# Four of nine taps of three depthwise 3x3 convolutions move from TensorE to VectorE in the overlapped stages

## Chip, cores and metric

The kernel runs on one core of a Trainium2 chip. The metric is the device time of one launch in microseconds (us); for the kernel before, the median of 3 runs is 12007.12 us (11998.74 to 12011.87).

## What is computed

The input is x, eight images of 64 channels and 64 x 64 pixels in float32. Four blocks follow one another. Each of the last two has parts that don't matter here; what matters are three depthwise 3x3 convolutions (one 3x3 filter for each channel):

```python
# block 0: attention over all 4096 pixels, then
out = conv3x3_depthwise(out, w2); out = relu(bn2(out)); out = bn3(conv1x1(out, w3)) + x
# block 1: two layers of attention in 8x8 windows, each with an MLP
# block 2: nine spatially weighted taps, a 1x9 convolution, a residual
# block 3: a selective scan (state space model) over four directions
xc = silu(conv3x3_depthwise(xi, conv_w) + conv_b)      # 128 channels
h = h * exp(dt * A) + dt * B * xc; y = sum(h * C)      # along 4096 pixels, 16 states, 4 directions
# block 3, last part: the channels in four groups i, each max-pooled by 2**i,
# each with a 3x3 depthwise convolution (mfr_w, mfr_b), upsampled, joined, then
out = gelu(conv1x1(joined, aggr_w) + aggr_b) * x
```

## The kernel before

Two images are handled together as a pair, on 128 partitions (2 images x 64 channels); a tile of one pair is 128 x 4096 and is worked on in eight chunks of 512 columns (8 rows of 64 pixels). There are four pairs. For each, the *front* (L1282) computes blocks 0 to 2 and, in `scan_sources` (L1645), the inputs of the scan; the *scan* (L1713) follows; the *back* (L1882) makes the output from the scan's result, the pyramid of pooled convolutions being its second half.

The stages overlap. The front of pair 0 runs by itself (about 0 to 1530 us). Then, beside the scan of pair p, run the back of pair p-1 and the front of pair p+1. The scan of pair 3 has the back of pair 2 beside it, and the back of pair 3 partly beside it and partly behind it. The front and back are Python generators that yield a cost; `scans` records scan steps and takes from the generators in proportion. The program's order sets only the priorities: a scheduler puts the instructions on each engine's queue, each engine then works its queue in order.

A scan has 512 steps, each with two of the sixteen states of 512 columns. A step is: two row broadcasts by DMA (B and C, L1801); on POOL (GpSimd) a product of 128 x 1024 (`vd<-B,du`, L1809); on ScalarE (ACT) two exponentials (`dad`, L1831) and copies of the carried ends (L1842); on VectorE (DVE) two scans (`hd` or `dad`, L1834); the product with C, on POOL or DVE (L1845, L1848); and on TensorE (PE) two sums (`yd<-vd`, L1860), each over half of PE's columns. Eight steps share two products of input rows (`pdd`, `pbc`, L1771 and L1779).

A depthwise tap on PE is a product with a diagonal 128 x 128 matrix made by `spread_taps` (L1249). `taps_sum` (L1269) makes a chunk: taps 0 to n-1 on PE into one PSUM bank, the others as multiply-adds on DVE into the same bank:

```python
            if t < n:
                nc.tensor.matmul(dst, lhsT=diag[:, t], rhs=src, start=(t == 0), stop=stop and t == n - 1)
            else:
                nc.vector.scalar_tensor_tensor(dst, src, wt[:, t : t + 1], dst, ALU.mult, ALU.add)
```

It is used at three places. In `layer0` (L1364) the bank `cacc` is read by ACT (L1366), goes through a 1x1 product on PE (`pw`, L1368), ACT again, and is added to X on DVE (L1371). In `scan_sources` (L1672), for each of the two images of a pair, the bank `xacc` is read by ACT with Silu (L1674), copied to XT (L1675), and stored by DMA (L1676). At both, n is 5 while a front is alone (pair 0) and 9 in the three others. In the back (L1975), the first level of the pyramid of pairs 0 to 2 has all nine taps on PE, with the 1x1 weights `agT` folded into the diagonal matrices, so that the bank `pa` holds that level's part of the joined sum directly; three products with the upsampled other levels follow (L1979), then Gelu on ACT (L1986), two DVE instructions (L1987, L1988), and the store. For the last pair (`alone` in `back`) all nine taps are on DVE. PSUM banks come from rings of three: `f` for the front and back, `da` for the scan; in the last scan the back alternates between the two.

Of the kernel before, what the change touches and what calls it, by code (L numbers as in the profile page):

```python
# [9 lines left out]
F32 = mybir.dt.float32  # L10
AF = mybir.ActivationFunctionType
ALU = mybir.AluOpType
# [5 lines left out]
P = 128  # L18
# [4 lines left out]
TAPS = 9  # L23
# [1136 lines left out]
class _Direct:  # L1160
# [127 lines left out]
    def layer0(self, p):  # L1288


        nc, tc, w, net, half = self.nc, self.tc, self.w, self.net, self.HALF
        X = self.flat("X")
        nc.sync.dma_start(X, self.net.x[2 * p : 2 * p + 2].rearrange("b c h w -> (b c) (h w)"))
        att = self.padded("att")
        VT = self.flat("VT").rearrange("p (t c) -> p t c", c=P)

        def at(rows, t):
            return X[rows, t * P : (t + 1) * P]

        with self.work("w0") as wk:  # L1300
            for g in range(8):
                pv = self.bank("pval", (P, 4, P))
                nc.tensor.matmul(pv, lhsT=net.ones[0:1, :], rhs=net.b1row.rearrange("o a c -> o (a c)").unsqueeze(1).to_broadcast([1, 4, P]), start=True, stop=False)
                for j in range(4):
                    nc.tensor.matmul(pv[:, j, :], lhsT=at(slice(0, P), 4 * g + j), rhs=net.w1bd, start=False, stop=(j == 3))
                nc.scalar.activation(VT[:, 4 * g : 4 * g + 4, :], pv, AF.Relu)
                yield 3

            parts = wk.tile([P, 2, 32, NCH], F32, name="parts", tag="parts", bufs=1)
            self.dense = 1  # L1310
            for jc in range(NCH):
                po = self.total("po")

                def weigh(t, es):
                    for im in range(2):
                        nc.tensor.matmul(  # L1316
                            po[half[im]], lhsT=VT[:, t, half[im]], rhs=es[im], start=(t == 0), stop=(t == 31)
                        )

                last = None  # L1320
                for t in range(32):
                    ss = [self.bank(f"s{im}") for im in range(2)]
                    for im in range(2):
                        nc.tensor.matmul(  # L1324
                            ss[im], lhsT=at(half[im], t), rhs=X[half[im], jc * CH : (jc + 1) * CH], start=True, stop=True
                        )
                    es = []
                    for im in range(2):
                        e = wk.tile([P, CH], F32, name="e", tag="e", bufs=5)
                        nc.scalar.activation(  # L1330
                            e, ss[im], AF.Exp, scale=C**-0.5, accum_out=parts[:, im, t, jc : jc + 1]
                        )
                        es.append(e)
                    if last is not None:
                        weigh(*last)
                    last = (t, es)
                    yield 3.6
                weigh(*last)
                nc.vector.tensor_copy(self.rows(att, jc), self.img(po))  # L1339

            self.dense = 0
            sums = net.sums[:, p]
            nc.vector.tensor_reduce(sums, parts, AX.X, ALU.add)
            rec = wk.tile([P, 2, 32], F32, name="rec", tag="rec", bufs=1)
            nc.vector.reciprocal(rec, sums)
            for g in range(8):
                pr = self.bank("prec")
                for j in range(4):
                    for im in range(2):
                        nc.tensor.matmul(  # L1350
                            pr[half[im], j * P : (j + 1) * P],
                            lhsT=rec[:, im, 4 * g + j : 4 * g + j + 1].to_broadcast([P, 64]),
                            rhs=w["ident"],
                            start=True,
                            stop=True,
                        )
                d = self.rows(att, g)
                nc.vector.tensor_tensor(d, d, self.img(pr), ALU.mult)
                yield 3
        with self.work("w0b") as wk:  # L1360
            diag = self.spread_taps(wk, w["dw2"])
            for c in range(NCH):
                acc = self.bank("cacc", (P, 8, 64))
                yield from self.taps_sum(acc, diag, att, 8 * c, 1.56, wt=w["dw2"], n=5 if self.alone else TAPS)  # L1364
                cv = wk.tile([P, 8, 64], F32, name="cv", tag="cv")
                nc.scalar.activation(cv, acc, AF.Relu, scale=net.bn23[:, 0:1], bias=net.bn23[:, 1:2])  # L1366
                pw = self.bank("pw")
                nc.tensor.matmul(pw, lhsT=w["w3bd"], rhs=cv, start=True, stop=True)  # L1368
                nc.scalar.activation(pw, pw, AF.Identity, scale=net.bn23[:, 2:3], bias=net.bn23[:, 3:4])
                x = X[:, c * CH : (c + 1) * CH]  # L1370
                nc.vector.tensor_tensor(x, x, pw, ALU.add)  # L1371
                yield 2.25
        return X
# [271 lines left out]
    def scan_sources(self, p, X2):  # L1645

        nc, tc, w, net, half = self.nc, self.tc, self.w, self.net, self.HALF
        x2 = self.memory("x2")
        with tc.tile_pool(name="w3", bufs=2) as wk:
            H = self.flat("H3")  # L1650
            diag = self.spread_taps(wk, w["cw"])
# [7 lines left out]
            for im in range(2):  # L1659
                xc, xt, zs = self.memory("xc"), self.memory("xt"), self.memory("zs")  # L1660
                pad = self.padded("XI")
                for c in range(NCH):
                    pi = self.bank("pi")
                    nc.tensor.matmul(
                        pi, lhsT=w["inT"][half[im], 0:P], rhs=H[half[im], c * CH : (c + 1) * CH], start=True, stop=True
# [3 lines left out]
                XT = self.flat("XT").rearrange("p (w h) -> p h w", h=64)  # L1669
                for c in range(NCH):  # L1670
                    acc = self.bank("xacc", (P, 8, 64))
                    yield from self.taps_sum(acc, diag, pad, 8 * c, 1.5, wt=w["cw"], n=5 if self.alone else TAPS)  # L1672
                    cv = wk.tile([P, 8, 64], F32, name="xcv", tag="xz")
                    nc.scalar.activation(cv, acc, AF.Silu, bias=w["cb"])  # L1674
                    last = nc.scalar.activation(XT[:, 8 * c : 8 * c + 8, :], cv, AF.Copy)  # L1675
                    nc.scalar.dma_start(xc[:, c * CH : (c + 1) * CH], cv.rearrange("p a b -> p (a b)"))  # L1676
                    yield 1.4
# [5 lines left out]
                for c in range(NCH):  # L1683
# [3 lines left out]
                        lhsT=w["inT"][half[im], P : 2 * P],  # L1687
# [194 lines left out]
    def back(self, p):  # L1882
# [3 lines left out]
        F = self.padded("F")  # L1886
# [23 lines left out]
        with tc.tile_pool(name="w5", bufs=1) as wk:  # L1910
            prev, n, ups = F, 64, []
            alone = p == B // 2 - 1
            for i in range(1, 4):
# [40 lines left out]
                ups.append(up)  # L1954
                prev = pool
                yield 7
            ab = w["aggr_b"]
            if not alone:
                near = self.spread_taps(wk, w["mw"][:, 0, :], w["agT"][:, 0, :])
                pm = self.bank("pmb")  # L1960
                nc.tensor.matmul(pm[:, 0:1], lhsT=w["agT"][:, 0, :], rhs=w["mb"][:, 0:1], start=True, stop=True)
                ab = wk.tile([P, 1], F32, name="ab", tag="ab")
                nc.vector.tensor_tensor(ab, pm[:, 0:1], w["aggr_b"], ALU.add)
            for c in range(NCH):
                cols = slice(c * CH, (c + 1) * CH)
                if alone:
                    acc = self.bank("sacc", (P, 8, 64))
                    yield from self.dwconv(acc, F, 8 * c, 8, w["mw"][:, 0, :], w["mb"][:, 0:1])
                    S = wk.tile([P, 8, 64], F32, name="S", tag="S", bufs=2)
                    nc.scalar.activation(S, acc, AF.Copy)  # L1970
                    pa = self.bank("pa", (P, 8, 64))
                    nc.tensor.matmul(pa, lhsT=w["agT"][:, 0, :], rhs=S, start=True, stop=False)  # L1972
                else:
                    pa = self.bank("pa", (P, 8, 64))
                    yield from self.taps_sum(pa, near, F, 8 * c, 1.5, stop=False)  # L1975
                for i in range(1, 4):
                    k = 2**i
                    r = 8 // k
                    nc.tensor.matmul(  # L1979
                        pa,  # L1980
                        lhsT=w["agT"][:, i, :],
                        rhs=ups[i - 1][:, c * r : (c + 1) * r, :].unsqueeze(2).to_broadcast([P, r, k, 64]),
                        start=False,
                        stop=(i == 3),
                    )
                last = nc.scalar.activation(pa, pa, AF.Gelu, bias=ab)  # L1986
                nc.vector.tensor_tensor(pa, pa, self.rows(F, c), ALU.mult)  # L1987
                nc.vector.tensor_tensor(X[:, cols], X[:, cols], pa.rearrange("p a b -> p (a b)"), ALU.add)  # L1988
                nc.sync.dma_start(out[:, cols], X[:, cols])
                yield 3.5  # L1990
# [52 lines left out]
```

## Time and profile before

| | us |
|---|---|
| median of 3 runs | 12007.12 |
| the profiled execution | 12011.7 |
| its span, first to last instruction | 12009.9 |
| front of pair 0 alone | about 0 to 1530 |
| layer-0 convolution, fronts 1, 2, 3 | 2533.6 to 2629.0; 5463.5 to 5563.1; 8346.1 to 8444.6 |
| scan-source convolutions, fronts 1, 2, 3 (two images each) | 3890.5 to 4088.3; 6778.4 to 6970.6; 9660.1 to 9853.8 |
| first pyramid level, backs of pairs 0, 1, 2 | 4462.2 to 4546.3; 7348.9 to 7433.0; 10533.2 to 10688.1 |
| last sum of the scan of pair 3 | 11894 |

Three rows of the page show the course of the span in 40 slices of 300 us, busy tenths for an engine and granted tenths of full clock for PEclk:

```profile
PE   9977999998888779998788978999877986675656
...
DVE  0033367767778474666777555666777748989998
...
PEclk9998989999989889999998989999999987786677
```

A group's line reads: line, engine, operation, written tile <- read tiles, shapes and count | busy us in sum, mean ns of one | idle time of that engine just before, and what ended it. An fp32 product appears as two MATMUL records. Granted clock is the share of TensorE's full clock.

### The profile page before, as it was taken

To read this page: it belongs to the slowest core of one execution; us is meant where nothing else is said; L and a number is where in the kernel's file an instruction comes from. 1 tells how busy PE (TensorE), PEld (TensorE's weight loads), DVE (VectorE), ACT (ScalarE), POOL (GpSimd) and SP (SyncE) were. 2 spreads that over 40 slices of the span, in tenths; PEclk is the share of its full clock that TensorE was granted. 3 is DMA by queue.
4 is the path that set the end of the run, shared out by engine and by line. 5 is a ranking of instruction groups with operands and counts; after the bars stand their busy time and mean duration, and the time that the engine had idled before them with its cause. 6 is when DMAs were issued, how large, how long until landed. Compare 5 with 4: busy or idle time off the path is not lost. (4 is left out here: it accounts for less than half of the span.)

```text
span 12009.9 us, 161406 instructions
## 1 busy us (share of the span) xinstructions
PE 9980.9 (83%) x56180; PEld 3350.9 (28%) x56180; DVE 7806.3 (65%) x8943; ACT 6974.8 (58%) x16029; POOL 7487.9 (62%) x3843
## 2 busy tenths in 40 slices
PE   9977999998888779998788978999877986675656
PEld 2244322233322223223342223222333221121111
DVE  0033367767778474666777555666777748989998
ACT  5555367756665555665665554665666455565554
POOL 0000066668778573666877774566778758888994
PEclk9998989999989889999998989999999987786677
DMA  0000055545445553444444553444444446666663
GB/s 20 1 2 4 33 154 150 148 132 145 134 127 161 157 175 91 136 142 121 147 118 133 150 175 113 127 136 134 135 131 139 128 153 191 185 194 200 206 202 122
DMA packets 779773, 1577.04 MB, mean 131 GB/s; under 512 B 89280, under 2 KB 89408, under 8 KB 778176
## 3 DMA queue, kind: packets, MB, share of 16 engines
q1 hardware_dynamic: 736320, 1443.18, 40.2%
q10 hardware_dynamic: 42624, 123.44, 3.6%
q8 instruction: 444, 7.27, 0.3%
q14 instruction: 385, 3.15, 0.1%
HBM read 1197.16 MB, written 100.66 MB: 108 GB/s over the span
## 5 line engine op out<-in xcount | busy, mean ns | idle before, releaser
L1809 POOL TENSOR_TENSOR vd<-B,du 128x1024 f32<-128x1024 f32 x2048 | 4792.9, 2358 | 2802.6 <-DMA B<-rows 1797.4
L1860 PE MATMUL yd<-vd,pack 128*64 128x512 f32 x8192 | 2705.0, 705 | 668.8 <-POOL vd L1848 466.5
L1831 ACT ACTIVATE dad<-du,As 128x512 f32<-128x512 f32 x4096 | 2721.3, 682 | 697.0 <-DVE hd L1834 331.6
L1834 DVE TENSOR_TENSOR_SCAN hd<-dad,carry,vd 128x512 f32<-128x512 f32 x1989 | 2491.0, 1269 | 529.7 <-ACT dad L1831 471.4
L1848 POOL TENSOR_TENSOR vd<-hd,C 128x512 f32<-128x512 f32 x1293 | 1642.0, 1274 | 818.0 <-DVE hd L1834 816.8
L1834 DVE TENSOR_TENSOR_SCAN dad<-dad,carry,vd 128x512 f32<-128x512 f32 x1595 | 2011.5, 1276 | 184.4 <-ACT dad L1831 181.2
L1845 POOL TENSOR_TENSOR vd<-hd,C 128x1024 f32<-128x1024 f32 x488 | 1149.9, 2356 | 765.9 <-DVE hd L1834 362.7
L1330 ACT ACTIVATE e<-s 128x512 f32<-128x512 f32 x2048 | 1200.1, 591 | 623.4 <-PE s L1324 621.7
L1324 PE MATMUL s<-X 64*128 64x512 f32 x4096 | 1455.6, 647 | 85.5 <-ACT e L1330 66.0
L1848 DVE TENSOR_TENSOR vd<-dad,C 128x512 f32<-128x512 f32 x1827 | 1212.4, 677 | 130.0 <-ACT carry L1842 98.2
L1860 PEld LDWEIGHTS yd<-vd,pack 128*64 128x64 f32 x8192 | 617.5, 154 | 2403.4 <-issue 1152.3
L1316 PE MATMUL po<-e,VT 128*64 128x512 f32 x4096 | 1210.3, 627 | 19.3 <-ACT e L1330 16.2
L1842 ACT ACTIVATE carry<-dad 128x1 f32<-128x1 f32 x1597 | 267.1, 169 | 776.8 <-DVE dad L1834 684.0
L1324 PEld LDWEIGHTS s<-X 64*128 64x128 f32 x4096 | 400.6, 187 | 1129.3 <-issue 840.7
L1842 ACT ACTIVATE carry<-hd 128x1 f32<-128x1 f32 (+1 forms) x1559 | 308.8, 201 | 660.3 <-DVE hd L1834 649.4
L1483 PE MATMUL w_av<-wide,vals 64*32 64x64 f32 x16384 | 494.9, 227 | 116.6 <-DVE w_oc L1512 77.8
L1483 PEld LDWEIGHTS w_av<-wide,vals 64*32 64x32 f32 x16384 | 406.9, 113 | 272.2 <-issue 151.7
L1316 PEld LDWEIGHTS po<-e,VT 128*64 128x64 f32 x4096 | 235.7, 136 | 850.5 <-issue 570.8
L1243 PE MATMUL pv<-n_sq,pack 128*128 128x512 f32 x576 | 347.7, 687 | 148.8 <-ACT n_sq L1241 138.6
L1494 PE MATMUL w_av<-wide,each 64*32 64x128 f32 x8192 | 465.5, 282 | 6.6 <-issue 6.6
L1471 ACT ACTIVATE wide<-wide 128x512 f32<-128x512 f32 x512 | 311.5, 628 | 269.9 <-DVE wide L1470 269.9
L1339 DVE COPY att<-po 128x512 f32<-128x512 f32 x32 | 22.0, 686 | 682.8 <-PE po L1316 682.3
(259 smaller groups left out, 11629.5 us busy)
## 6 DMA issues: line engine op xcount, KB each, us to landing
B<-rows SPq DMA_DIRECT2D x2048, 256.0 KB, 3.6
C<-rows SPq DMA_DIRECT2D x2048, 256.0 KB, 3.6
du<-du SPq DMA_DIRECT2D x384, 512.0 KB, 5.8
du<-du ACTq DMA_DIRECT2D x128, 512.0 KB, 5.1
xs<-xt SPq DMA_DIRECT2D x128, 256.0 KB, 3.9
xs<-xc SPq DMA_DIRECT2D x128, 256.0 KB, 3.7
xc<-xcv ACTq DMA_DIRECT2D x64, 256.0 KB, 2.0
xt<-XT ACTq DMA_DIRECT2D x32, 512.0 KB, 6.1
```

What stands on the lines that cost most here:

```text
L1316: nc.tensor.matmul(po[half[im]], lhsT=VT[:, t, half[im]], rhs=es[im], start=(t == 0), stop=(t == 31))
L1324: nc.tensor.matmul(ss[im], lhsT=at(half[im], t), rhs=X[half[im], jc * CH : (jc + 1) * CH], start=True, stop=True)
L1330: nc.scalar.activation(e, ss[im], AF.Exp, scale=C**-0.5, accum_out=parts[:, im, t, jc : jc + 1])
L1483: nc.tensor.matmul(self.av[rows, 0, x % 4 + j], lhsT=net.vals[half[im], x + j, 4 * g + h], rhs=es[g][half[im], j, h], tile_position=(64 * ...
L1494: nc.tensor.matmul(self.av[rows, 1, x % 4 : x % 4 + 2], lhsT=net.each[half[im], 32 - HD - HD * h : 64 - HD - HD * h], rhs=es[g][half[im], ...
L1809: self.nc.gpsimd.tensor_tensor(v, self.twice(st["B"]), self.units[i // 8]["du"][:, :, 1], ALU.mult)
L1831: nc.scalar.activation(da, u["du"][:, j, 0], AF.Exp, scale=net.As[:, k, n : n + 1])
L1834: nc.vector.tensor_tensor_scan(along(to), along(da), along(v[:, j]), first, ALU.mult, ALU.add)
L1842: nc.scalar.activation(cs, ends, AF.Copy)
L1845: st["w"] = nc.gpsimd.tensor_tensor(v, h, self.twice(CC), ALU.mult)
L1848: m = engine.tensor_tensor(v[:, j], hs[j], CC, ALU.mult)
L1860: m = nc.tensor.matmul(u["y"][self.HALF[j]], lhsT=w["fold"], rhs=st["v"][:, j], start=(i % 8 == 0), stop=(i % 8 == 7))
```

## The change

At the first two places n becomes 5 in all fronts: taps 0 to 4 stay on PE, taps 5 to 8 become multiply-adds on DVE. In the backs of pairs 0 to 2 the first level's taps 0 to 3 are made on DVE in a tile S in SBUF (a share of `big`, one buffer), the bias `mb` going in with the first; taps 4 to 8 stay on PE with the folded matrices; S goes through one product with `agT` into the same bank. The bias of the folded form (one product `pmb` and one small addition) goes. Costs yielded to `scans` stay the same in sum.

```diff
-                yield from self.taps_sum(acc, diag, att, 8 * c, 1.56, wt=w["dw2"], n=5 if self.alone else TAPS)
+                yield from self.taps_sum(acc, diag, att, 8 * c, 1.56, wt=w["dw2"], n=5)
...
-                    yield from self.taps_sum(acc, diag, pad, 8 * c, 1.5, wt=w["cw"], n=5 if self.alone else TAPS)
+                    yield from self.taps_sum(acc, diag, pad, 8 * c, 1.5, wt=w["cw"], n=5)
...
-            ab = w["aggr_b"]
             if not alone:
                 near = self.spread_taps(wk, w["mw"][:, 0, :], w["agT"][:, 0, :])
-                pm = self.bank("pmb")
-                nc.tensor.matmul(pm[:, 0:1], lhsT=w["agT"][:, 0, :], rhs=w["mb"][:, 0:1], start=True, stop=True)
-                ab = wk.tile([P, 1], F32, name="ab", tag="ab")
-                nc.vector.tensor_tensor(ab, pm[:, 0:1], w["aggr_b"], ALU.add)
...
                 else:
+                    S = self.img(self.share(big, 3))
                     pa = self.bank("pa", (P, 8, 64))
-                    yield from self.taps_sum(pa, near, F, 8 * c, 1.5, stop=False)
+                    for t in range(TAPS):
+                        tap = F[:, 8 * c + t // 3 : 8 * c + t // 3 + 8, t % 3 : t % 3 + 64]
+                        wt = w["mw"][:, 0, t : t + 1]
+                        if t == 0:
+                            nc.vector.tensor_scalar(S, tap, wt, w["mb"][:, 0:1], ALU.mult, ALU.add)
+                        elif t < 4:
+                            nc.vector.scalar_tensor_tensor(S, tap, wt, S, ALU.mult, ALU.add)
+                        else:
+                            nc.tensor.matmul(pa, lhsT=near[:, t], rhs=tap, start=(t == 4), stop=False)
+                        if t % 3 == 2:
+                            yield 1.5
+                    nc.tensor.matmul(pa, lhsT=w["agT"][:, 0, :], rhs=S, start=False, stop=False)
...
-                last = nc.scalar.activation(pa, pa, AF.Gelu, bias=ab)
+                last = nc.scalar.activation(pa, pa, AF.Gelu, bias=w["aggr_b"])
```

## The prediction

> **What bounds the kernel now.** I read the page first (busy shares), then the busy time of the stretches in which the edited convolutions run, then the waits in one of them, and then stretches of window attention, which tell what a scan step costs when it must share TensorE.
>
> ```profile
> PE 9980.9 (83%) x56180; PEld 3350.9 (28%) x56180; DVE 7806.3 (65%) x8943; ACT 6974.8 (58%) x16029; POOL 7487.9 (62%) x3843
> ```
>
> TensorE (PE) is the busiest engine, but 83% of a span with several stages does not say where it is the limit. The edited stretches do (columns: start and end, length, then busy us and instructions of each engine, granted clock, DMA share, GB/s). In order: the layer-0 convolution of the second front (2531 to 2630) and the third (5463 to 5564), the two images of a scan-source convolution (6778 on), and the pyramid's first level in the back of pair 1 (7347) and of pair 2 (10530).
>
> ```profile
> core 0: us, PE busy (x) PEld busy (x) DVE busy (x) ACT busy (x) POOL busy (x), PEclk, DMA share, GB/s
> 2531.00:2630.00 99.00, 94.33 (x225) 33.45 (x221) 44.52 (x47) 35.54 (x76) 62.10 (x30) 0.97 0.36 105
> 5463.00:5564.00 101.00, 93.69 (x212) 33.84 (x212) 48.20 (x49) 38.32 (x83) 56.30 (x28) 0.97 0.38 110
> ...
> 6778.00:6858.00 80.00, 80.00 (x202) 29.98 (x200) 36.10 (x35) 46.42 (x75) 45.77 (x23) 1.00 0.45 132
> 6898.00:6971.00 73.00, 73.00 (x183) 28.37 (x181) 21.19 (x22) 33.56 (x52) 32.01 (x16) 1.00 0.27 80
> ...
> 7347.00:7434.00 87.00, 86.63 (x205) 37.64 (x203) 31.07 (x41) 25.71 (x42) 8.66 (x6) 1.00 0.25 75
> 10530.00:10688.00 158.00, 142.33 (x370) 46.29 (x370) 137.34 (x155) 110.48 (x220) 127.41 (x69) 0.98 0.61 187
> ```
>
> In all but the last, PE works 93 to 100% and VectorE (DVE) under half. The last is another regime: DVE 87%, POOL 81%, PE 90%. The waits between 6778 and 6971 say the same; the scan's own sums queue behind taps (engine and line that waited, for whom, us in total, times, longest):
>
> ```profile
> PEld xacc L1275 <- issue: 70.4, 259, 0.8
> DVE xs L1878 <- PE yd L1860: 60.3, 3, 27.9
> ACT xcv L1674 <- PE xacc L1275: 50.7, 8, 7.1
> ```
>
> **Prices.** A full product is two records; in the pyramid 12 products make a chunk, and the gelu product L1987 recurs every 10.30 us there: 0.858 us a product. A scan step's two sums run side by side (yd records start in pairs 0.43 us apart), so a step costs PE 0.86 us, with 1/8 of its two input products 1.07. A step costs DVE about 2.8 us (third front: 48.2 less 4.8 for L1371, over 15.5 steps) and POOL 4.2 (2.36, and 2.36 or 1.27 in turn). Taps on DVE are in the first front's rows: 0.756 each, four in a row 3.13 us (L1277, source in SBUF, accumulator in PSUM).
>
> **Layer-0 convolution (L1364), three fronts.** Removed: 8 chunks x 4 taps x 0.858 = 27.5 us of PE in each; added: 8 x 3.13 = 25 us of DVE. The instruction order of the two builds (counting yd sums between the first and last tap) shows a side effect: the convolution spans 13 scan steps before and 29 after in the second front, 12 and 24 in the other two; by the end of the first attention block both builds stand at the same step. So 16, 12, 12 steps move forward out of the layer norm and first block. In the new stretch PE no longer rules: with 29 steps DVE needs 114 us by its listed order (59 scans at 1.2, 32 taps, the rest at 0.6), POOL 29 x 4.2 = 121; with 24, DVE 107. I take 120, 108 and 108 for 99, 101 and 99: +37 us. What are the moved steps worth where they left? The trace has the experiment: the same block of eight window rows with different numbers of steps (four yd records to a step):
>
> ```profile
> core 0: us, PE busy (x) PEld busy (x) DVE busy (x), PEclk, DMA share, GB/s
> 2725.00:2989.50 264.50, 62.36 (x208) 13.03 (x206) 6.60 (x7) 0.92 0.48 141
> ...
> 5655.50:5905.60 250.10, 59.12 (x194) 12.93 (x194) 6.87 (x7) 0.94 0.47 137
> 6062.60:6299.40 236.80, 52.50 (x162) 11.20 (x162) 7.09 (x6) 0.95 0.42 118
> ```
>
> From 208 to 162 records is 11.5 steps and 27.7 us, 2.4 each; from 194 to 162, 1.7. At 2.0, 40 steps give back 80 us. Net -43. Ends: 1.07 a step (PE's share alone) gives -6; 2.4 gives -59.
>
> **Scan-source convolution (L1672), six images.** Per image PE falls by 27.5 us to 52.5 in the first stretch and 45.5 in the second; DVE rises by 25, to 61 in the first. ACT gets more table loads: the order of the new build alternates Silu and Exp more often, 34 more loads over the six images at 1.28 us (the ACT_TABLE_LOAD rows), 7 an image: 54 and 41 in this front. No engine is full any more. The trace's stretches without a full engine run their largest engine at about 86% (window block at 3149: PE 217.8 of 252.7). So 61 / 0.86 = 71 for 80 us, and in the second image, with DVE, the largest, at 46 to 53 in the three fronts (52 taken), 60 for 73: -9 and -13, three times, -66. Ends: 0, if the chain PE, DVE, ACT is as slow as PE was, and -120, if the largest engine fills.
>
> **Pyramid, first level, backs of pairs 0 and 1 (L1975).** 12 products a chunk become 9: 7.72 for 10.30 us, 8 chunks, -20.6 each. The single S buffer adds a wait: the first tap of the next chunk waits for the product on S, then DVE needs 2.77 us (0.54 for the first, between the rows of L436 at 256 and 1024 elements, 3 x 0.74 from L438), while PE still has three upsampled products and five taps, 6.9 us. That hides it, except in the second and fourth chunk, where up to seven scan instructions are listed between its taps: about 2 us each. -17 each, -34, less 3 for the port below: -31. Ends -40 and -8. The dropped bias product and its 4.0 us wait (L1963) I cost at nothing: PE sets the start of the stretch.
>
> **Back of pair 2, in the last scan.** PE was not the limit, so 24 products less buy nothing; 8 x 2.77 = 22 us of DVE are added where it is 87% busy. And here S matters: three taps in four read F and S, both in SBUF, and the first writes SBUF from SBUF. The row nearest to that is the pooling maximum, both inputs in SBUF:
>
> ```profile
> L1918 DVE TENSOR_TENSOR big<-pool x8: 285/1779/2717, 4426.5 to 11937.7; 128x512 f32<-128x512 f32 x4, 128x128 f32<-128x128 f32 x4
> ```
>
> The 512-element form takes 0.69 us with POOL idle (at 11924) and 2.71 beside three POOL products (at 4426), each of which also grew from 2.36 to 2.5 to 2.8. The Trainium skill (SBUF — State Buffer, "SBUF: two separate sides") has the reason, an exclusive lock on a port pair shared by DVE and POOL, taken by DVE instructions with two SBUF inputs or in a two-port mode; whoever starts first keeps it to the end. By the rule a tap arriving at random waits half a POOL instruction four times in five, 0.8 us: 32 x 0.8 = 26. By the row, 2.0 each: 65. Scans stand between many taps, so I take 1.0: 32. Then (22 + 32) x 0.87 = +48. Ends +15 and +85. The taps into PSUM have one SBUF input and are free of this: L1619, of that kind, stays at 0.75 us beside POOL.
>
> A second rule speaks against the change: TensorE: Matmul & The Clock Gate, "What's actually happening": the clock is full only while PE was recently busy. The row: granted 1.00 in the saturated stretches, 0.92 to 0.95 in the window blocks (85% busy), 0.67 between 10700 and 11500 (58%). With 0.87 the first scan-source stretch needs 52.5 / 0.87 = 60 us of PE, still under 71; by the rule, no idle window, 52.5. Neither changes the sum; up to +20 goes into the range.
>
> **Sum.** -43 - 66 - 31 + 48 = -92. The profiled execution took 12011.7 us (span 12009.9), so 11919.7; the median of the runs shown is 4.6 below that execution: 11915.
>
> **The rivals.** *Given back* (0.12 for within 0.2%, some 24 us, about what a measurement here can tell): moved steps are worth 1.07, the scan-source chain takes its 80 us: -6 + 0 - 31 + 48 = +11, 12018. For it: ACT waits and table loads. Against: DVE and ACT stand under 60% there. *Half* (0.14): cover as computed, but only half of the first two gains, -37, 11970.
>
> *DVE's queue held by TensorE* (0.18, slower): each chunk's first DVE tap waits for its fifth product, and behind it in DVE's queue stand scans, for which POOL and then PE's sums wait. In the first front, with nothing else on PE, DVE waited 1.2 us a chunk (L1277 <- PE xacc). With sums between the products, which wait for POOL up to 6.6 us, I take 2.5: 72 chunks x 2.5 = 180, -92 + 180, about 12100. It decides from 1.3 us a chunk (92 / 72), and is measurable from 1.6. Against it: the scheduler lists scans between taps, and three banks let a chunk's products run ahead.
>
> That the change does nothing is excluded by the order: 4 of 9 tap products are gone from 72 chunks, 3 net in the pyramid. The first front and last back are untouched. *More* (0.06): largest engines fill, 11820.
>
> The likeliest case, 11915, has 0.50, with 11860 to 11965 its own. Faster 0.50 + 0.14 + 0.06 = 0.70, same 0.12, slower 0.18. The range 11830 to 12040 leaves out the slower rival and most of "more".
>
> **What would show it.** Right: the scan-source stretches at 58 to 74 us with PE under 85%; layer-0 stretches longer but the blocks after them 20 to 30 us shorter; the chunk period of the first two pyramids 7.7 us; in the third, S taps of 1.5 us and more. Wrong: DVE idle on PE cacc or PE xacc of over 100 us in sum, or window blocks that don't shrink.

## The result, and the profile after

The changed kernel takes 11917.2 us (median of 4 runs, 11911.3 to 11936.5) against 12004.4 us (4 runs, 11998.7 to 12011.9): ratio 0.9928, 95% interval 0.9916 to 0.9941, some 87 us less. The prediction said 11915. The sum was right to a few us; its terms were not, and the experiments below show which.

First the busy shares of the page of the changed kernel, then the layer-0 convolution of fronts 1 and 2 and the pyramid's first level in the backs of pairs 1 and 2, from the first tap to the last. The columns are those of the same view before.

```profile
span 11913.0 us, 160345 instructions
...
PE 9652.2 (81%) x55454; PEld 3219.2 (27%) x55454; DVE 8095.3 (68%) x9324; ACT 7056.3 (59%) x16085; POOL 7496.5 (63%) x3843
```

```profile
core 0: us, PE busy (x) PEld busy (x) DVE busy (x) ACT busy (x) POOL busy (x), PEclk, DMA share, GB/s
2523.40:2657.50 134.10, 98.21 (x242) 28.80 (x242) 119.25 (x132) 70.84 (x158) 132.19 (x65) 0.86 0.57 174
5405.00:5535.30 130.30, 92.09 (x226) 31.70 (x226) 109.82 (x122) 64.23 (x131) 113.04 (x56) 0.85 0.54 162
...
7257.50:7324.30 66.80, 63.99 (x148) 27.64 (x148) 47.81 (x64) 27.53 (x38) 6.13 (x5) 1.00 0.29 90
10409.70:10587.60 177.90, 131.71 (x314) 41.15 (x312) 165.76 (x173) 103.75 (x200) 126.99 (x66) 0.87 0.52 159
```

Read each against its row before. Layer 0 (first two rows) became longer, 134 and 130 us for 95 and 100, and PE is no longer full: 73% and 71%, at a granted clock of 0.86 and 0.85. The pyramid of pair 1 fell from 84 to 66.8 us with PE still 96% busy. The pyramid of pair 2 grew from 155 to 178, with DVE at 93%.

The scan sources of front 2 are cut at the same three points in both kernels: the first image's convolution, the stretch between the images (the projections `pz` and `pi` and their ScalarE steps), and the second image's convolution. Before, then after:

```profile
core 0: us, PE busy (x) PEld busy (x) DVE busy (x) ACT busy (x) POOL busy (x), PEclk, DMA share, GB/s
6778.40:6855.10 76.70, 76.70 (x194) 29.27 (x193) 33.73 (x32) 43.63 (x72) 42.88 (x21) 1.00 0.45 131
6855.10:6896.00 40.90, 31.84 (x53) 9.96 (x53) 8.87 (x13) 25.50 (x37) 19.17 (x10) 0.65 0.69 217
6896.00:6970.60 74.60, 74.60 (x183) 29.23 (x184) 22.30 (x22) 35.08 (x55) 32.92 (x16) 0.98 0.27 79
```

```profile
6714.10:6766.80 52.70, 50.96 (x133) 17.81 (x132) 47.67 (x56) 39.03 (x60) 35.13 (x18) 1.00 0.59 176
6766.80:6819.50 52.70, 38.02 (x48) 9.63 (x48) 17.10 (x20) 34.98 (x51) 26.93 (x14) 0.52 0.44 147
6819.50:6868.00 48.50, 48.50 (x125) 17.49 (x124) 43.96 (x53) 42.82 (x60) 32.94 (x16) 1.00 0.48 148
```

The convolutions fell by 24 and 26 us, about the 27.5 us of products that left PE. PE is still the full engine in them (97 and 100%), at full clock; DVE now stands at 90 and 91%. The stretch between the images did not shrink: it grew by 12 us, at a lower clock.

The window blocks that stood for the price of a scan step now hold fewer steps (160 and 146 records for 208 and 194) and are shorter, 236 and 221 us for 264 and 250. Then three of the longest waits of the scan sources of front 2 (6682 to 6868). The 60 us of `xs` waiting for PE's sums are down to 2 between first and last tap. The second line is idle time of the weight loads between products; it fell with their number, 133 for 259, and is 0.27 us each as before:

```profile
core 0: us, PE busy (x) PEld busy (x) DVE busy (x), PEclk, DMA share, GB/s
2732.50:2968.70 236.20, 48.96 (x160) 10.40 (x160) 5.23 (x5) 0.93 0.41 122
5622.90:5844.40 221.50, 43.95 (x146) 9.57 (x146) 5.03 (x5) 0.95 0.37 107
```

```profile
POOL vd L1845 <- DVE hd L1834: 45.5, 7, 11.1
PEld xacc L1275 <- issue: 36.0, 133, 0.8
DVE hd L1834 <- ACT dad L1831: 32.8, 17, 9.0
```

The same points of both traces give the course of the gain, each between instructions that both kernels have, before then after:

| | front 1 | front 2 | front 3 | sum of differences |
|---|---|---|---|---|
| layer 0 convolution and first attention block (last attention sum to last projection) | 471.8, 460.3 | 456.0, 453.5 | 448.9, 457.6 | -5.3 |
| scan sources (their diagonals to the back's first norm) | 310.4, 287.3 | 298.0, 268.0 | 299.6, 268.4 | -84.3 |

| | pair 0 | pair 1 | pair 2 |
|---|---|---|---|
| back, first norm to first pyramid product | 329.4, 335.9 | 333.0, 335.9 | 634.0, 647.7 |
| first pyramid level | 84.1, 66.8 | 84.1, 66.8 | 154.9, 177.9 |

The -84 of the scan sources, cut further (three fronts together, us):

| | before | after | difference |
|---|---|---|---|
| from the diagonals to the first tap | 189.1 | 191.1 | +2.0 |
| the six convolutions, first tap to last | 454.9 | 309.3 | -145.6 |
| between the two images | 128.8 | 155.1 | +26.3 |
| from the last tap to the back's first norm | 135.2 | 168.2 | +33.0 |

The backs of pairs 0 and 1 give -25, that of pair 2 costs +37. What is left of the 97 us between the two spans lies in stretches nobody edited: -13 between the first attention block and the scan sources, and some -6 elsewhere.

### The profile page after: what moved, and what is told of

It reads as the page before. It is cut to its first block, busy times and chain, and to the rows that moved or that the text cites. A ratio compares the mean times of both kernels' runs of the same rounds, so it can differ in the third digit from the quotient of the medians.

```text
span 11913.0 us, 160345 instructions
## 1 busy us (share of the span) xinstructions
PE 9652.2 (81%) x55454; PEld 3219.2 (27%) x55454; DVE 8095.3 (68%) x9324; ACT 7056.3 (59%) x16085; POOL 7496.5 (63%) x3843
## 5 line engine op out<-in xcount | busy, mean ns | idle before, releaser
L1860 PE MATMUL yd<-vd,pack 128*64 128x512 f32 x8192 | 2667.3, 702 | 749.2 <-POOL vd L1848 508.4
```

Of the source, the lines that this page charges most:

```text
L1860: m = nc.tensor.matmul(u["y"][self.HALF[j]], lhsT=w["fold"], rhs=st["v"][:, j], start=(i % 8 == 0), stop=(i % 8 == 7))
```

## The experiments

**The parts one by one.** Each kernel is the one before with part of the change.

```diff
# e1_layer0_only
-  yield from self.taps_sum(acc, diag, att, 8 * c, 1.56, wt=w["dw2"], n=5 if self.alone else TAPS)
+  yield from self.taps_sum(acc, diag, att, 8 * c, 1.56, wt=w["dw2"], n=5)
# e2_sources_only
-  yield from self.taps_sum(acc, diag, pad, 8 * c, 1.5, wt=w["cw"], n=5 if self.alone else TAPS)
+  yield from self.taps_sum(acc, diag, pad, 8 * c, 1.5, wt=w["cw"], n=5)
# e3_pyramid_only: the changed back, both taps_sum as before
# e4_pyramid_01: as e3, but the back of pair 2 keeps the folded form
+  elif p == B // 2 - 2:
+      pa = self.bank("pa", (P, 8, 64))
+      yield from self.taps_sum(pa, near, F, 8 * c, 1.5, stop=False)
```

> Only the layer-0 convolution is divided (5 products and 4 VectorE taps in all fronts). By the prediction's term: -43 us, ratio 0.9964. By the theory read from the two traces (the stretch grows by about 32 us in each front, the attention block after it shrinks by about as much): -5 us, within -20 to +10, ratio 0.998 to 1.001. If the small changes in stretches that nobody edited belong to this part, it would be nearer to -25.

> Only the scan-source convolution is divided. By the prediction's term: -66 us, ratio 0.9945. By the two traces: -84 us, ratio 0.993, nearly the whole gain of the change. If the parts need one another (a gain in one only because another has moved scan steps), it would be under half of that.

> Only the first pyramid level in the backs of pairs 0 to 2 is changed. By the prediction: -31 + 48 = +17 us, ratio 1.0014. By the two traces: -25 + 40 = +15 us, ratio 1.0012; the chunk period of pairs 0 and 1 falls from 10.30 to about 7.7 us, and the taps on S in pair 2 take about 1.7 us each where those of pairs 0 and 1 take 0.75.

> The pyramid is changed in the backs of pairs 0 and 1 alone; pair 2, beside the last scan, keeps the nine folded products. By the prediction: -31 us, ratio 0.9974. By the traces: -25 us, ratio 0.998. Against the run with all three pairs it tells the price of pair 2: +40 to +48 us if that is VectorE's extra work and the shared port, under 10 if pair 2 was free.

Measured on one chip, before 12002.5 us:

| | median us | ratio | 95% interval |
|---|---|---|---|
| layer 0 only | 11998.9 | 0.9993 | 0.9985 to 1.0001 |
| scan sources only | 11915.0 | 0.9923 | 0.9910 to 0.9937 |
| pyramid, pairs 0 to 2 | 12015.5 | 1.0009 | 1.0001 to 1.0018 |
| pyramid, pairs 0 and 1 | 11981.0 | 0.9981 | 0.9973 to 0.9989 |

The deviations of the first three add to -0.75%, the change has -0.72%: the parts are additive within the intervals. The scan sources alone are the whole gain. Layer 0 gains nothing that can be measured, and in the pyramid pair 2 costs 12015.5 - 11981.0 = 34 us, more than pairs 0 and 1 gain.

**Why layer 0 gives nothing.** In the layer-0 stretch of the changed kernel PE waits, though it has less to do. The longest waits (engine and line that waited, for whom, us in sum, times, longest), then PE's own timeline of 36 us of it (start, length, instructions, and in brackets the idle time before):

```profile
PEld pw L1368 <- ACT cv L1366: 30.6, 6, 7.1
PE pw L1368 <- ACT cv L1366: 25.3, 6, 6.3
```

```profile
5446.70 2.08 PE L1368 MATMUL pw<-cv,pack 128*128 128x512 f32 x2 [6.23 <-ACT cv L1366]
5448.57 5.63 PE L1275 MATMUL cacc<-att,diag 128*128 128x512 f32 x10
5454.13 6.22 PE L1860 MATMUL yd<-vd,pack 128*64 128x512 f32 x26
5460.28 1.13 PE L1771 MATMUL pdd<-xs,xdt 128*128 128x512 f32 x2
5467.66 2.08 PE L1368 MATMUL pw<-cv,pack 128*128 128x512 f32 x2 [6.25 <-ACT cv L1366]
5469.53 5.39 PE L1275 MATMUL cacc<-att,diag 128*128 128x512 f32 x10
```

The chunk shown takes 21 us; over the stretch they average 16 (130.3 / 8). The 1x1 product `pw` stands at the head of PE's queue and waits 6.2 us for `cv`, which waits for the four taps on DVE, between which the scheduler has put scans. Only then come the next chunk's five products. And the idle time costs twice: from 5444.1 to 5450.9 the granted clock is 0.50, and `pw` takes 2.08 us for its two records, where one without idle time before it, in the run with the fourth bank below, takes 1.03. The three banks of the ring would hold `cacc`, `pw` and one more `cacc`, and a divided chunk keeps its bank longer. That is a theory of the ring; one bank more tests it. Bank `acc` is idle in this stretch.

```diff
# e7_layer0_fourth_bank, on top of e1; e11_bank_nine has the bank alone, with nine products
-  acc = self.bank("cacc", (P, 8, 64))
+  acc = (self.total if c % 2 and not self.alone else self.bank)("cacc", (P, 8, 64))
```

> Layer 0 divided, with every second chunk's bank from a fourth PSUM bank that is idle in this stretch. In the instruction order the convolution now spans 15, 12 and 12 scan steps, as before the change, instead of 29, 24 and 24: no step moves. Theory that the ring of three banks kept a chunk's chain (products, taps, ScalarE, product, ScalarE, VectorE) from overlapping, so that scan steps filled in: the stretch takes about 80 us for 99, the attention block stays as before, in sum -40 to -60 us, ratio 0.995 to 0.997. Rival, that the freed TensorE time can't be used since VectorE and POOL take its place: stretch near 100, ratio 0.999 to 1.000, as without the fourth bank.

> Control for the fourth bank: layer 0 undivided, nine products, with the fourth bank; nothing else changed. If the bank helps only because the divided chain is long, TensorE stays saturated and the time is that of the kernel before (ratio 0.999 to 1.001). If the bank by itself was the gain of the run before, ratio near 0.992.

Measured: 11913.9 us against 12007.1 with the fourth bank, ratio 0.9921 (0.9908 to 0.9935). The control, the bank with nine products, has 12003.8 against 12004.7, ratio 1.0002 (0.9993 to 1.0010). So neither the bank nor the division does anything alone, and both together take 93 us: well beyond the 40 to 60 expected. The ring of three is thus what kept the division from paying. Whether the fourth bank acts while the kernel runs, or by the order that the scheduler makes with it, these runs do not separate: it moves the scan steps too (yd records in the three stretches 54, 49 and 49 before; 132, 120 and 120 in the changed kernel; 62, 60 and 60 here). Two stretches of that run:

```profile
2533.00:2614.00 81.00, 66.96 (x164) 22.58 (x164) 70.03 (x83) 40.66 (x86) 63.15 (x31) 0.94 0.51 148
5436.80:5511.10 74.30, 63.05 (x158) 22.15 (x160) 68.57 (x81) 37.40 (x80) 58.59 (x29) 0.95 0.49 150
```

80.2, 74.3 and 74.3 us from first tap to last, for 95.4, 99.6 and 98.5 before: 65 us. DVE is the fullest engine in the second, at 92%, PE at 85%. The norm between convolution and first block takes 22 us less in the three fronts than before. It holds fewer scan steps (216 yd records for 238, five or six steps); at the prediction's 2.0 us a step that is about half of it, an estimate, and the rest is open.

**Pair 2 and the shared port.** First the taps on S in the changed kernel (min/median/max ns, all three backs), then those of the run in which pair 2's taps accumulate in PSUM:

```profile
L1977 DVE SCALAR_TENSOR_TENSOR big<-F,pack,big x72: 719/752/2859, 4389.9 to 10573.5; 128x512 f32<-128x512 f32 x72
```

```profile
L1978 DVE SCALAR_TENSOR_TENSOR big<-F,pack,big x48: 719/748/753, 4431.5 to 7384.3; 128x512 f32<-128x512 f32 x48
L1978 DVE SCALAR_TENSOR_TENSOR sacc<-F,pack,sacc x24: 725/744/756, 10479.8 to 10624.6; 128x512 f32<-128x512 f32 x24
```

```diff
# e6_taps_psum, on top of e3; also at the two DVE taps: T in place of S
   S = self.img(self.share(big, 3))
+  T = self.bank("sacc", (P, 8, 64)) if p == B // 2 - 2 else S
...
+  if T is not S:
+      nc.scalar.activation(S, T, AF.Copy)
   nc.tensor.matmul(pa, lhsT=w["agT"][:, 0, :], rhs=S, start=False, stop=False)
```

> As the run with the pyramid alone, but in pair 2 the four VectorE taps accumulate in a PSUM bank (one SBUF input, no two-port form) and ScalarE copies the sum to S. VectorE's listed work grows by 0.3 us a chunk. Theory of the shared port: taps fall from 1.7 to 0.75 us, POOL's products return from 2.44 to 2.36 us, and pair 2 costs some 20 us less: ratio to before about 0.999, against 1.0009. Rival, that pair 2 pays for VectorE work as such: the same time or up to 5 us more, ratio 1.001 to 1.0015.

Measured: 11990.4 against 12007.1, ratio 0.9985 (0.9977 to 0.9994), where the pyramid alone had 1.0009 (1.0001 to 1.0018): about 29 us less, where some 20 were expected, though DVE has as many instructions and ACT eight copies more. In the pyramid-alone run the groups of pair 2's stretch (10498 to 10674) read

```profile
L1809 POOL TENSOR_TENSOR vd<-B,du 128x1024 f32<-128x1024 f32 x38 | 92.5, 2449 | 43.0 <-DMA du<-du 17.5 <-DMA B<-rows 12.4 <-PE yd L1860 9.5
...
L1977 DVE SCALAR_TENSOR_TENSOR big<-F,pack,big 128x512 f32<-128x512 f32 x21 | 30.7, 1460 | 0.2
...
L1982 PE MATMUL pa<-big,pack 128*128 128x512 f32 x16 | 12.2, 851 | 21.7 <-DVE big L1977 21.7
...
L1975 DVE TENSOR_SCALAR big<-F,pack 128x512 f32<-128x512 f32 x7 | 9.4, 1338 | 0.0
```

A tap takes 1.46 us for 0.75 and the first 1.34 for 0.54, and POOL's products 2.45 for 2.36. With the sum in PSUM, the taps are at 0.74, the first at 0.81, the product at 2.35. So most of pair 2's cost goes with the second input in SBUF beside a busy GpSimd; DVE's added work as such is the small rest. The traces show the delay, not the lock by which the prediction explains it. The shorter taps make about 22 us of DVE time (24 x 0.72 and 8 x 0.53, an estimate); the order of instructions differs too, and what the other 7 are is open. The single buffer S is not the rival: DVE waited 0.0 us before the first taps.

**More taps to DVE, and the gains together.**

```diff
# e8_sources_four, on the kernel before
-  ..., wt=w["cw"], n=5 if self.alone else TAPS)
+  ..., wt=w["cw"], n=5 if self.alone else 4)
# e5_sources_pyramid_01 = e2 and e4; e9_all_gains = e5 and e7
# e10_sources_fourth_bank: as e9, and the fourth bank for xacc too
-  acc = self.bank("xacc", (P, 8, 64))
+  acc = (self.total if c % 2 and not self.alone else self.bank)("xacc", (P, 8, 64))
```

> Only the scan sources, with four products on TensorE and five taps on VectorE in the overlapped fronts. If TensorE is still the limit there, each further product gives what the first four gave (87 us / 192 products = 0.45 us): 48 more, -22 us, about -109. If VectorE and ScalarE now share the limit, no gain or a loss: -87 to -60.

> The parts that gained alone: the scan-source convolution and the pyramid of pairs 0 and 1; layer 0 and pair 2 as before. If parts add up, -87 - 21 = -108 us, ratio 0.991, some 20 us below the changed kernel. If they share one slack, nearer to -88, as the sources alone.

> The scan sources and the pyramid of pairs 0 and 1 divided, and layer 0 divided with the fourth bank; pair 2 as before. If parts add up: -87 - 21 - 93 = -201 us, ratio 0.983, about 11805. If the gains of layer 0 and of the sources draw on one slack of the stage, well above that, 11850 or more.

> As e9_all_gains, with the fourth bank for every second chunk of the scan sources too. Theory that the ring of three banks limits this chain as well: 10 to 40 us less than e9_all_gains. Rival, that ScalarE's table loads and VectorE set the pace here (the order shows steps at 24 instead of 22 in the stretch, so little moved): within 10 us of it.

| | median us | before us | ratio | 95% interval |
|---|---|---|---|---|
| sources, four products | 11924.1 | 12007.1 | 0.9931 | 0.9917 to 0.9944 |
| sources, pyramid 0 and 1 | 11897.9 | 12007.1 | 0.9911 | 0.9897 to 0.9924 |
| and layer 0 with fourth bank | 11792.8 | 12004.7 | 0.9823 | 0.9810 to 0.9837 |
| and fourth bank for the sources | 11802.3 | 12004.7 | 0.9827 | 0.9814 to 0.9841 |

A fifth tap on DVE in the scan sources brings no more than the fourth (0.9931 and 0.9923, intervals over each other), and its trace says why. The first convolution of front 2:

```profile
6742.40:6792.30 49.90, 43.67 (x113) 14.85 (x114) 49.44 (x63) 39.65 (x60) 32.78 (x16) 0.98 0.54 161
```

DVE is at 99%, PE at 88%. The six convolutions took 298 us, where they take 309 in the run with the scan sources only, and 19 more were lost between and behind them: five products and four taps are about balanced. A fourth bank brings nothing there. The gains of the three places add up: 11793 us, 212 below the kernel before and some 124 below the changed one (by medians of different groups of runs).

## Why the prediction was right, and where it was not

- *Layer 0, -43: failed.* Measured alone: -4 us (ratio 0.9985 to 1.0001). The step that failed is "I take 120, 108 and 108 for 99, 101 and 99: +37 us". From first to last tap it was 134, 130 and 131 against 95, 100 and 99, +101. The sizes came from the busy time of DVE and POOL, and only in the first of the fronts is POOL's what the stretch took (132 of 134 us). In the others no engine was full (in front 2 DVE 110 and POOL 113 of 130 us); the chain through three banks set the pace, 16 us a chunk. The prediction took the moved scan steps as given and did not ask why the scheduler moved them; with the fourth bank they hardly move. Its other half was right in kind: the shorter blocks and the norm before them gave back 106 us (80 forecast). The blocks alone fell by 28, 29 and 21.
- *Scan sources, -66: right in kind, wrong in both directions.* Measured -87 alone, -84 between the traces. The step "No engine is full any more" failed: PE stayed full, and the convolutions came to 53 and 49 us in front 2, not 71 and 60. The prediction's own figure for PE's work, 52.5 and 45.5, was the better forecast. DVE, which it put at 61 us, had 48 in the first image, because the shorter stretch also holds fewer scans (18 of them for 24). So the six convolutions gave 146 us, more than the 120 of the prediction's best end. What it put at nothing was the rest: 26 us were lost between the images and 33 behind them. There PE works at a granted clock of 0.52 for 0.65 (front 2) and waits for ScalarE; how much of the loss is clock and how much is ScalarE work left over from the convolution no run separates.
- *Pyramid, pairs 0 and 1, -31: right in mechanism, a little too much.* -17.3 each in the stretch, where -17 was forecast, but 3 and 6.5 were lost ahead of it; -21 by the run alone, -25 by the traces.
- *Pair 2, +48: right in mechanism, a little high.* +37 by the traces, +34 by the runs. The port's part was put at 32 of 54 us of DVE time; taking it away gave about 29 us.
- *The clock: harmless where the prediction looked, missed elsewhere.* The prediction lowered the clock inside the scan-source convolutions, and found that this does not change the sum. There it stayed at 0.96 to 1.00. But it fell in layer 0, from 0.97 to 0.85 in front 2, where a product after 6.2 us of idle PE took twice its time, and between the two images, from 0.65 to 0.52. How much of the shortfall is clock no run separates.
- *The slower rival* (DVE's queue held by TensorE) did not decide, but its mirror image ruled layer 0: TensorE's queue held by the taps on DVE (through `cv`), 25 us in one stretch against 5.3 us for DVE waiting on `cacc`. In the scan sources DVE waited 4 to 5 us on `xacc` in a front.

That the total fell on the forecast is chance in part: 39 us too much were expected of layer 0 and 6 to 10 of pairs 0 and 1, against some 20 too little of the sources, 11 to 14 too dark a view of pair 2, and small gains in stretches not edited. The sources' term is itself such a sum: 80 us too little for the convolutions, some 60 for losses that were not counted. Of the signs named beforehand, the pyramids' (7.7 us a chunk, slow taps on S in pair 2) and the shorter blocks came; the scan-source convolutions, at 49 to 54 us with PE at 89 to 100%, lie outside the 58 to 74 us under 85% that it named as right.

## What to carry to other kernels

Work moved from a full engine to an idle one lengthens a dependent chain; what it returns can then depend on how many chunks the buffers let run at once, as in layer 0, so count the banks of the ring beside the engine time. Cut a stretch at the same instructions in both traces before reading a busy share or a clock from it: a window that takes in the next step shows the mean of two regimes. Before pricing an instruction on VectorE, look whether it reads two SBUF operands beside a busy GpSimd; here an accumulator in PSUM took the delay away. Split an edit that touches several places by place: here one place held the gain, one was neutral for want of a bank, and one pair of three cost more than the two others won.

## What the runs showed of the hardware

An fp32 multiply-add of 128 x 512 with both inputs in SBUF took up to 2.86 us beside GpSimd products of 2.36 us, 0.75 without; and the GpSimd product grew to 2.45. TensorE's clock reacts within a stretch: a product of two records took 2.08 us after 6.2 us of idle time, and 1.03 without idle time in the run with the fourth bank. There, where PE is 85% busy, the granted clock is 0.95, in the same stretch with 71% it is 0.85. But the busy share alone does not give the clock: between the two images PE is 72% busy and the clock is 0.52. In the changed kernel it was at half from 6768.5 to 6819.7, though PE worked from 6800.5 to 6820.3 without a pause. Most products there (`pi`, `yd`) use 64 of the 128 rows or columns, while the convolutions' full products ran at 0.96 to 1.00; but the window blocks, with products of 64 rows and 32 columns among them, ran at 0.93 to 0.95, so smaller products alone do not explain it. The cause is open.
